# Gate scores of the second batch: as multiplying sums on VectorE from h, in place of matrix products on TensorE

## The chip, the cores and the metric

The kernel runs on one core of a Trainium2 chip. The metric is the device time of one launch, in microseconds (us), as the median of several runs. A core has TensorE (matrix products, written to PSUM), VectorE, ScalarE and GpSimd (elementwise work), SyncE (which issues transfers) and 16 DMA engines that all queues share. Every engine works through its own instructions strictly in order and waits on semaphores for the others. In the views of the profile, PE is TensorE, PEld its weight load, DVE VectorE, ACT ScalarE, POOL GpSimd and SP SyncE.

## What is computed

The input is x of shape (2, 1024, 256): two batches of 1024 rows, all in float32. There are two layers, each with a residual and a layer normalisation without weights behind it: a causal attention with one head of width 256, and a block with a 16-head causal attention (head width 128, rotary embedding) and a mixture of four experts. The part that matters here, cut from the reference (a, h, m of the second block):

```python
h = hidden_states + a
m = _moe(_layernorm(h, ln2_w, ln2_b), w_gate, we1, be1, we2, be2)
...
x = h.reshape(-1, d)                       # the normalised rows
raw = jax.nn.softmax(x @ w_gate, axis=-1)  # w_gate: 256 x 4
top_vals, top_idx = jax.lax.top_k(raw, TOP_K)
w = jax.nn.softmax(top_vals, axis=-1)
comb = jnp.zeros((t, E), x.dtype).at[jnp.arange(t)[:, None], top_idx].add(w)
hmid = jax.nn.gelu(jnp.einsum('td,edi->tei', x, we1) + be1[None], approximate=False)
eout = jnp.einsum('tei,eid->ted', hmid, we2) + be2[None]
out = jnp.einsum('te,ted->td', comb, eout)
```

So each of the 2048 rows has four gate scores, one for each expert; its two best experts are chosen by them, and the weights of the experts are held in comb (zero for the two that are not chosen). All four experts are computed for every row.

## The kernel before

Rows are worked in tiles of 128 (on the 128 partitions), eight tiles to a batch b. Half a batch (four tiles) is called j. The rows of h stand in one large tile (hx in the profile, 16 tiles of 128x256); the transposed, normalised rows stand in xT (called x2T in this part), features on the partitions.

**Order.** The body does not emit instructions at once. Each piece of work is a named call (`hidden 1 0 0` is `hidden` for batch 1, half 0, expert 0) that is put into a list; at the end the table MOVES (L28 to 299) takes single names out and puts them ahead of other names, and the list is then emitted. No scheduler works behind this: the order of the list is the order in every engine's queue. `at(s + 5, f)` puts a call into the step s + 5 of the attention's rows, of which s is the first of the last sixteen.

**The mixture of experts.** For half a batch the calls are: `m_stats` and `m_rstd` (mean, variance and 1/deviation of each row of h), `m_norm` (the normalised rows; on VectorE for batch 1, L498), `m_transposed` (four transposes on TensorE to PSUM, then ln2_w and ln2_b applied on the way to x2T: feature half c = 0 by ScalarE, L509, c = 1 by VectorE, L507), `gate_products`, `gate`, `gate_best`, `gate_weights` (from scores to comb), `hidden` for each expert (eight products of 512 columns into two PSUM banks, each then taken by a Gelu on ScalarE, L1693), `all_of` (16 products with we2 for one expert and four tiles, each tile then added to h with its weight from comb, VectorE, L1717), `m_bias` (the experts' second biases by the same instruction from SBUF, VectorE, L1672) and `m_residual` (adds x1 to h, GpSimd, L1577).

`hidden` uses two PSUM banks in turn, so that the next `hidden` can begin only when the Gelu of the one before has emptied the bank. ScalarE has to load a table when it goes from Exp or Ln to Gelu and back (ACT_TABLE_LOAD).

**The gate.** `gate_products` (L1586) makes, for each tile, two products of the transposed rows with w_gate, 128 columns by 4, and copies the scores of two tiles from PSUM with VectorE (L1601). `gate` (L1617) takes the largest score of a row, subtracts it and takes the exponential on ScalarE (L1625); `gate_best` finds the best and second best expert, and for the second takes another exponential on ScalarE (L1652); `gate_weights` writes comb. For batch 1 the four `gate_products` stand in two groups: tiles 0 to 3 behind `hidden 0 1 0`, tiles 4 to 7 behind `hidden 0 1 3`, and behind these come `gate 1`, `gate_best 1 0`, `gate_best 1 1`, `hidden 1 0 0`, `all_of 0 1 2`, `gate_weights 1`, `all_of 0 1 3`, `hidden 1 0 1`.

**The end of the attention.** The rotary tables stand in rope_sb (128 x 2 x 1024) and are used by GpSimd (L834 to L836) up to the last projection. For the last attention rows, VectorE transposes blocks of the softmax rows (L662), SyncE gathers them with 16 transfers of 128 KB (L673) into the tile pT, and TensorE multiplies them with the values (L1209). On GpSimd's own DMA queue, `load_second` (L1509) loads the last expert's we2 (256 KB, L1511) and be2, spread to all partitions (512 KB, L1513).

Of the kernel before, what the change touches and what calls it, by code (L numbers as in the profile page):

```python
# [12 lines left out]
F32 = mybir.dt.float32  # L13
AF = mybir.ActivationFunctionType
ALU = mybir.AluOpType
# [3 lines left out]
P = 128  # L19
# [13 lines left out]
    ("o_stats 1 0 0.1.2.3", "hidden 1 1 1"),  # L33
    ("hidden 1 0 3", "o_finish 0 0 0.1.2.3"),
    ("hidden 1 0 0", "all_of 0 1 2"),
    ("gate_products 1 6.7", "gate_products 1 4.5"),
    ("m_norm 1 1", "m_residual 0 0.1.2.3"),
    ("m_rstd 1 4.5.6.7", "m_norm 1 1"),
# [273 lines left out]
def kernel(  # L312
# [27 lines left out]
    nc = tc.nc  # L340
    B, S, D = x.shape
    DC = D // P
    NT = S // P
# [6 lines left out]
    E, I = be1.shape  # L350
# [63 lines left out]
    mpool = ctx.enter_context(tc.tile_pool(name="mpool", bufs=1))  # L414
# [49 lines left out]
    rope_sb = const.tile([P, 2, S], F32, name="rope_sb")  # L464
# [9 lines left out]
    h = hx.rearrange("p (n d) -> p n d", d=D)  # L474
# [648 lines left out]
    class RowB:  # L1123
# [45 lines left out]
        def place(self, j):  # L1169
            return (blocks_b if units.index(self.u) else blocks_a)[j]  # L1170
# [99 lines left out]
    def at(step, f, *args):  # L1270
        place(fills, step, f, args)
# [4 lines left out]
    def mid(step, f, *args):  # L1276
        place(mids, step, f, args)
# [113 lines left out]
    for k, (g, b) in enumerate(pairs):  # L1391
# [3 lines left out]
        wide = 0 < k < len(pairs) - 1  # L1395
# [90 lines left out]
    pools = {}  # L1486
# [52 lines left out]
    mv_h = [mpool.tile([P, NT, 2], F32, tag=f"mvh{b}", name="mvh") for b in range(B)]  # L1539
    rstd_h = [mpool.tile([P, NT], F32, tag=f"rsh{b}", name="rsh") for b in range(B)]  # L1540
# [3 lines left out]
    def table():  # L1544

        if other:
            nc.scalar.preload_act_table_set(TABLE)
            other.clear()
# [34 lines left out]

    pgs = {}

    def gate_products(b, tiles):  # L1586

        if tiles[0] == 0:
            pgs[b] = small.tile([P, NT, E], F32, tag="lg", name="lg", bufs=2)
        pg = ps_tr.tile([P, 512], F32, tag="tr", name="pg")  # L1590
        for i in tiles:
            for c in range(DC):
                nc.tensor.matmul(
                    pg[:, ts(i, E)],
                    lhsT=x2T[:, c, ds(b * S + i * P, P)],
                    rhs=wgate_sb[:, c, :],
                    start=(c == 0),
                    stop=(c == DC - 1),
                )
        lo, n = tiles[0], len(tiles)  # L1600
        nc.vector.tensor_copy(  # L1601
            pgs[b][:, lo : lo + n, :],
            pg[:, lo * E : (lo + n) * E].rearrange("p (n e) -> p n e", e=E),
        )

    def t3(tag):
        return small.tile([P, NT, E], F32, tag=tag, name=tag, bufs=2)

    def t2(tag):
        return small.tile([P, NT], F32, tag=tag, name=tag, bufs=2)  # L1610

    def wide(v):
        return v.unsqueeze(2).to_broadcast([P, NT, E])
# [3 lines left out]
    def gate(b):  # L1617

        lg = pgs[b]
        m = t2("gm")  # L1620
        nc.vector.tensor_reduce(m, lg, AX.X, ALU.max)
        nc.vector.tensor_tensor(lg, lg, wide(m), ALU.subtract)
        raw = t3("raw_g")
        table()
        nc.scalar.activation(raw, lg, AF.Exp)  # L1625
        raws[b] = raw
# [129 lines left out]
    s = A0 + (len(units) - 2) * NT  # L1756
    ST0, ST1, NM0, NM1 = 0, 2, 1, 3
    MT, GP0, H0 = (5, 6, 7, 8), (9, 9, 10, 11), 8
    GT = (11, 11, 12, 13)
    at(s + ST0, m_stats, 0, J0)  # L1760
    at(s + ST1, m_stats, 0, J1)
    at(s + NM0, m_rstd, 0, J0)
# [5 lines left out]
    for k in range(4):  # L1768
        at(s + GP0[k], gate_products, 0, (2 * k, 2 * k + 1))
    mid(s + H0, hidden, 0, 0, 0)  # L1770
    at(s + GT[0], gate, 0)
    at(s + GT[1], gate_best, 0, 0)
    at(s + GT[2], gate_best, 0, 1)
    at(s + GT[3], gate_weights, 0)
    for k in range(3):
# [27 lines left out]
    do(all_of, 0, 0, 2)  # L1803
    do(hidden, 0, 1, 0)
    do(gate_products, 1, (0, 1))
    do(gate_products, 1, (2, 3))
    do(all_of, 0, 0, 3)
    do(steps[end - 1].output, END)
# [19 lines left out]
    do(gate_products, 1, (4, 5))  # L1828
    do(gate_products, 1, (6, 7))
    do(gate, 1)  # L1830
    do(gate_best, 1, 0)
    do(gate_best, 1, 1)
# [84 lines left out]
```

## Time and profile before

| what | before |
|---|---|
| median of 3 runs | 1163.07 us (1158.52 to 1164.13) |
| the profiled execution | 1165.19 us, of which 1163.4 us is the span from the first to the last instruction |
| granted TensorE clock, mean | 0.994 of full speed |
| TensorE busy | 1133.0 us, 97% |
| VectorE busy | 852.5 us, 73% |
| GpSimd busy | 789.5 us, 68% |
| ScalarE busy | 648.7 us, 56% |
| gate products (L1593), both batches | 64 products of 128x128 by 128x4 |

Times within the profile count from the first instruction. The score products of the attention end at about 1031 us and its last output products at about 1078; the experts fill TensorE's time from 1039 on, and the calls of the gate for batch 1 lie between 1060 and 1106. A timeline line gives start, duration, engine, source line, operation, the tile written and those read with their shapes, how many instructions, and in brackets the idle time before and what ended it. The duration of several instructions reaches from the start of the first to the end of the last. A recorded duration overlaps the next instruction's start by up to 0.1 us, so that the distance of starts is the better price. A windows line gives, after the length of the window, the busy time of TensorE, its weight load, VectorE, ScalarE and GpSimd, each with a count in brackets, then the granted clock of TensorE, the mean busy share of the DMA engines, and GB/s. In the DMA view, q1 is SyncE's queue and q0 is GpSimd's.

### The profile page before, as it was taken

How to read it: one execution, taken by the hardware profiler on the slowest of the kernel's cores; microseconds unless marked ns; L12 is line 12 of the kernel's file. 1: busy time of each engine (PE TensorE's matmuls, PEld its weight loads, DVE VectorE, ACT ScalarE, POOL GpSimd, SP SyncE). 2: the span in 40 equal slices, each digit the busy share in tenths (PEclk: the TensorE clock that was granted, in tenths of full speed). 3: DMA queues.
4: the chain of work that ended last, by engine and by line, in shares of the span. 5: the costliest groups of instructions: out<-in, count | busy, mean ns of one | idle time of the engine just before them, and what ended most of it. 6: DMA issues, size and time to landing. Idle time of an engine off the chain costs nothing.

```text
span 1163.4 us, 15802 instructions
## 1 busy us (share of the span) xinstructions
PE 1133.0 (97%) x4628; PEld 718.6 (62%) x4628; DVE 852.5 (73%) x1813; ACT 648.7 (56%) x1228; POOL 789.5 (68%) x749
## 2 busy tenths in 40 slices
PE   8999989999999999999999999999999999999997
PEld 5666636656565656565757475756566656566765
DVE  5667797868686868687877778777868677575675
ACT  3333676665656565656566656565565656553444
POOL 4005999989897979697878868797989897002100
PEclk9999999999999999999999999999999999899999
DMA  6132465665546454555555545564555657405011
GB/s 187 36 88 57 117 174 140 135 138 125 127 113 130 107 138 110 118 122 131 119 125 131 131 112 131 132 138 115 132 129 128 148 121 180 106 15 145 1 37 36
DMA packets 243221, 133.89 MB, mean 115 GB/s; under 512 B 18908, under 2 KB 241184, under 8 KB 242368
## 3 DMA queue, kind: packets, MB, share of 16 engines
q1 hardware_dynamic: 238096, 123.02, 45.6%
q0 software_dynamic: 1776, 4.89, 1.6%
q10 hardware_dynamic: 3264, 4.98, 1.2%
q8 instruction: 37, 0.61, 0.2%
q14 instruction: 48, 0.39, 0.1%
HBM read 22.71 MB, written 4.19 MB: 23 GB/s over the span
## 4 chain that ended last, share of the span: by engine, by line
PE 87%; DVE 8%; DMA 2%; issue 1%; SPq 1%; ACT 1%; POOL 0%; DVEq 0%; ACTq 0%; POOLq 0%
PE sc L1143 19%; PE av L1209 19%; PE pa L919 10%; PE pa L1067 5%; PE pa L910 5%; PE pa L1685 5%; PE pe L1708 4%; PE pc L919 4%; PE pa L741 2%; PE sc L692 2%; PE pc L1067 2%; PE pc L910 2%; PE pa L599 1%; PE pa L586 1%; PE pa L1019 1%
## 5 line engine op out<-in xcount | busy, mean ns | idle before, releaser
L1160 ACT ACTIVATE pr<-pr,rs 128x128 f32<-128x128 f32 (+3 forms) x252 | 195.6, 778 | 188.9 <-DVE rs L1158 188.9
L1143 PE MATMUL sc<-Twk,Twq 128*128 128x512 f32 (+3 forms) x768 | 289.5, 487 | 4.3 <-ACT pr L624 4.3
L624 ACT ACTIVATE pr<-sc,nmx 128x640 f32<-128x640 f32 (+7 forms) x272 | 200.9, 739 | 154.4 <-DVE nmx L619 121.6
L1209 PE MATMUL av<-pT,vg 128*128 128x512 f32 (+3 forms) x768 | 271.0, 490 | 4.7 <-DMA pT<-pair_sb 2.4
L834 POOL TENSOR_TENSOR rot<-Twk,rope_sb 64x512 f32<-64x512 f32 x128 | 167.6, 1309 | 92.2 <-DVE Twk L952 70.0
L1209 PEld LDWEIGHTS av<-pT,vg 128*128 128x128 f32 x768 | 143.5, 191 | 128.6 <-issue 99.3
L619 DVE TENSOR_REDUCE nmx<-sc 128x1 f32<-128x640 f32 (+7 forms) x272 | 206.1, 758 | 9.4
L1143 PEld LDWEIGHTS sc<-Twk,Twq 128*128 128x128 f32 x768 | 135.6, 191 | 123.9 <-issue 108.7
L834 POOL TENSOR_TENSOR rot<-Twq,rope_sb 64x512 f32<-64x512 f32 x128 | 166.3, 1300 | 8.8
L617 DVE TENSOR_TENSOR sc<-sc,limit 128x128 f32<-128x128 f32 x272 | 79.2, 291 | 99.6 <-PE sc L1143 84.0
L662 DVE STREAM_TRANSPOSE x<-pr 128x640 f32<-128x640 f32 (+1 forms) x124 | 128.4, 1036 | 19.6 <-ACT pr L1160 11.9
L835 POOL TENSOR_TENSOR Twk<-Twk,rope_sb 128x512 f32<-128x512 f32 x64 | 85.8, 1341 | 5.0
L836 POOL TENSOR_TENSOR Twk<-Twk,rot 128x512 f32<-128x512 f32 x64 | 85.5, 1336 | 5.0
L835 POOL TENSOR_TENSOR Twq<-Twq,rope_sb 128x512 f32<-128x512 f32 x64 | 83.1, 1298 | 5.0
L836 POOL TENSOR_TENSOR Twq<-Twq,rot 128x512 f32<-128x512 f32 x64 | 82.0, 1281 | 5.0
L1577 POOL TENSOR_TENSOR hx<-hx,x 128x256 f32<-128x256 f32 x16 | 11.5, 745 | 90.1 <-DVE hx L1717 82.7
L662 DVE STREAM_TRANSPOSE pair_sb<-pr 128x128 f32<-128x128 f32 (+1 forms) x120 | 60.2, 502 | 8.0 <-ACT pr L1160 7.8
L1685 PE MATMUL pa<-xT,we_flat 128*128 128x512 f32 x128 | 59.6, 611 | 0.8 <-DVE hx L1029 0.8
L1076 DVE TENSOR_TENSOR hx<-hx,pa 128x512 f32<-128x512 f32 x70 | 46.6, 680 | 13.6 <-PE pa L1067 13.5
L1225 ACT ACTIVATE aT_sb<-av,par 128x512 f32<-128x512 f32 x64 | 43.8, 684 | 21.3 <-PE av L1209 19.8
L1708 PE MATMUL pe<-lent,hT 128*128 128x256 f32 x240 | 54.2, 379 | 0.0
L624 ACT ACTIVATION_READ_ACCUMULATOR pr<-sc,nmx 128x1 f32 x272 | 53.4, 196 | 0.0
(215 smaller groups left out, 1810.5 us busy)
## 6 DMA issues: line engine op xcount, KB each, us to landing
pT<-x SPq DMA_DIRECT2D x496, 128.0 KB, 2.7
pT<-pair_sb SPq DMA_DIRECT2D x480, 64.0 KB, 2.0
pT<-aT_sb SPq DMA_DIRECT2D x48, 128.0 KB, 2.7
pT<-za SPq DMA_DIRECT2D x48, 64.0 KB, 2.1
wk_g<-in_L_ffn_wk_dram SPq DMA_DIRECT2D x9, 256.0 KB, 3.0
wq_g<-in_L_ffn_wq_dram SPq DMA_DIRECT2D x9, 256.0 KB, 3.1
wv_g<-in_L_ffn_wv_dram SPq DMA_DIRECT2D x9, 256.0 KB, 3.1
wo_g<-in_L_ffn_wo_dram SPq DMA_DIRECT2D x9, 256.0 KB, 2.9
```

Source lines behind the costliest of these rows:

```text
L619: nc.vector.tensor_reduce(nmx, sc[:, :L], AX.X, ALU.max, negate=True)
L624: nc.scalar.activation(pr[:, :L], sc[:, :L], AF.Exp, bias=nmx, accum_out=sm)
L662: nc.vector.transpose(z[:, i % 4, :n, :], pr[:, : n * 32].rearrange("p (m s) -> p m s", s=32))
L834: nc.gpsimd.tensor_tensor(rot[lo, :], t[hi, cs], rope_sb[hi, 1, cs], ALU.mult)
L835: eng.tensor_tensor(t[:, cs], t[:, cs], rope_sb[:, 0, cs], ALU.mult)
L836: nc.gpsimd.tensor_tensor(t[:, cs], t[:, cs], rot, ALU.add)
L919: nc.tensor.matmul(pa, lhsT=w, rhs=x, start=start, stop=True, skip_group_check=True)
L1143: nc.tensor.matmul(sc[:, ds(n0, n)], lhsT=qT[:, ts(i, P)], rhs=kT[:, ds(n0, n)], start=True, stop=True,)
L1160: nc.scalar.activation(self.pr[:, :L], self.pr[:, :L], AF.Copy, scale=rs)
L1209: nc.tensor.matmul(cut(av), lhsT=vg[g, b][:, c, ts(hh, HD)], rhs=cut(pT[:, c, :]), start=(c == 0), stop=(c == i),)
L1685: nc.tensor.matmul(ph, lhsT=we1_sb[:, e, c, ts(m, P)], rhs=x2T[:, c, ds(k0 * P, 512)], start=(c == 0), stop=(c == DC - 1),)
L1708: nc.tensor.matmul(pe[:, ts(n, D)], lhsT=hTs[b, j, e][:, c, ts(k, P)], rhs=we2_sb[e][:, c, :], start=(c == 0), stop=(c == IC - 1),)
```

## The change

For batch 1, the scores of a row are made on VectorE from h itself. With g = ln2_w times w_gate (one row of 256 for each expert, on every partition) and c = the sum of ln2_b times w_gate, the score is rstd x (sum over d of (h - mean) x g) + c. The first factor and c are applied in `gate`. Batch 0 stays as it was.

```diff
+    ("gate_products 1 4.5", "m_residual 1 4.5.6.7"),
     ("gate_products 1 6.7", "gate_products 1 4.5"),
...
+    gw, g_raw = (rope_sb[:, k, :] for k in range(2))
+    cst = mpool.tile([P, E], F32, name="cst")
+    g_ln = []
+
+    def gate_loads():
+        nc.gpsimd.dma_start(g_raw, w_gate.rearrange("d e -> (d e)").partition_broadcast(P))
+        t = pools["l"].tile([P, 2, D], F32, tag="part", name="ln_rows", bufs=2)
+        for k, v in enumerate((ln2_w, ln2_b)):
+            nc.gpsimd.dma_start(t[:, k, :], v.partition_broadcast(P))
+        g_ln.append(t)
+
+    def gate_rows(e):
+        raw = g_raw.rearrange("p (d e) -> p e d", e=E)[:, e, :]
+        t = g_ln[0]
+        nc.gpsimd.tensor_tensor(gw[:, ts(e, D)], raw, t[:, 0, :], ALU.mult)
+
+        nc.vector.scalar_tensor_tensor(
+            g_junk, raw, 1.0, t[:, 1, :], ALU.mult, ALU.mult, accum_out=cst[:, e : e + 1]
+        )
+
+    g_junk = mpool.tile([P, D], F32, name="g_junk")
+
     def gate_products(b, tiles):
...
+        if b:
+
+            for i in tiles:
+                for e in range(E):
+                    nc.vector.scalar_tensor_tensor(
+                        g_junk, h[:, b * NT + i, :], mv_h[b][:, i, 0:1], gw[:, ts(e, D)],
+                        ALU.subtract, ALU.mult, accum_out=pgs[b][:, i, e : e + 1],
+                    )
+            return
...
     def gate(b):
 
         lg = pgs[b]
+        if b:
+            nc.vector.tensor_tensor(lg, lg, wide(rstd_h[b]), ALU.mult)
+            nc.vector.tensor_tensor(
+                lg, lg, cst.unsqueeze(1).to_broadcast([P, NT, E]), ALU.add
+            )
...
+    at(s + 5, gate_loads)
+    for e in range(E):
+        at(s + 7, gate_rows, e)
```

The order of the instructions of each engine, as built: TensorE loses 32 products. VectorE has 16 of the new instructions behind L1717 of `all_of 0 0 2` (tiles 0 to 3), and 16 behind L1717 of `all_of 0 1 1` (tiles 6, 7, 4, 5), ahead of L507 of `m_transposed 1 1 1` and of `gate 1`; each waits for the one before it, because all write g_junk. Before, L507 stood first there, and `m_residual 1 4.5.6.7`, which on GpSimd overwrites the h of those tiles, ran ahead of the gate products; it now stands behind them. The four sums for cst stand on VectorE behind the softmax maximum (L619) of the last full row of 1024, near 995 us in the profile before. GpSimd's three new loads (512, 128 and 128 KB) stand behind its `m_norm` of batch 0 (L498) and ahead of L1511 and L1513, its four products behind these. The loads write where the rotary tables were, and a buffer that the seven-product scheme used (tag part).

## Prediction, made before the changed kernel was run

> **What bounds the kernel.** I read the busy table and the chain of work that ended last, then the last 180 us on the timelines of TensorE, ScalarE and VectorE, the chain there, the DMA view in 2 us stretches, and the windows with the granted clock.
>
> ```profile
> PE 1133.0 (97%) x4628; PEld 718.6 (62%) x4628; DVE 852.5 (73%) x1813; ACT 648.7 (56%) x1228; POOL 789.5 (68%) x749
> ...
> PE 87%; DVE 8%; DMA 2%; issue 1%; SPq 1%; ACT 1%; POOL 0%; DVEq 0%; ACTq 0%; POOLq 0%
> ```
>
> TensorE is 97% busy and makes 87% of the chain. So a microsecond of TensorE counts in full, unless something else is then late. The second batch's gate scores stand on TensorE's timeline (start, duration):
>
> ```profile
> 1060.51 1.84 PE L1593 MATMUL pg<-wgate_sb,xT 128*128 128x4 f32 x16
> 1062.21 3.70 PE L1708 MATMUL pe<-lent,hT 128*128 128x256 f32 x16
> ...
> 1092.88 1.84 PE L1593 MATMUL pg<-wgate_sb,xT 128*128 128x4 f32 x16
> 1094.58 3.68 PE L1685 MATMUL pa<-xT,we_flat 128*128 128x512 f32 x8
> 1098.10 7.07 PE L1708 MATMUL pe<-lent,hT 128*128 128x256 f32 x32
> 1105.00 7.03 PE L1685 MATMUL pa<-xT,we_flat 128*128 128x512 f32 x16
> ```
>
> Each group holds TensorE for 1.70 us (1060.51 to 1062.21, 1092.88 to 1094.58), with no idle time behind it.
>
> **Removed: 2 x 1.70 = 3.40 us of TensorE**, and four copies of 0.17 us on VectorE, which sat waiting for them.
>
> **The new sums.** 32 SCALAR_TENSOR_TENSOR of 128x256 with an accumulated output. The trace has none with an accumulator. Nearest rows: eight of L1672 (128x256, two inputs in SBUF, each waiting for the one before, as the new ones do through the shared g_junk) take 4.00 us, 0.50 each; L1717 (one input in PSUM) is spaced by 0.415. ScalarE's accumulator is a record of its own, after which the next instruction starts 0.09 us later (992.33 to 992.42). I take 0.50 + 0.10 = **0.60**. Bounds: 0.415, and 0.50 + 0.42 = 0.92 if the sum were a pass of its own (L619 over 256 elements is 0.42). 0.60 is close to L1672, the same instruction but for the accumulator.
>
> A rule speaks against the change. The Trainium skill, "Vector Engine (DVE) Microarchitecture Reference", section "Points that are easy to get wrong", says that this instruction runs at half throughput with two SBUF sources that aren't bf16, as no read port is left for the accumulator. L1672, with two such sources but no accumulator, shows 0.50 against 0.415, no halving; whether the accumulator brings it, no row here shows. By the rule each would be some 0.25 to 0.30 us dearer, an estimate from that page, and 16 of them 4 to 5 us.
>
> In the second group, VectorE also runs m_norm 1 1 without GpSimd's additions beside it (four took 1.37 us at 1049.40, alone, and 2.20 at 1081.85, beside them); it then waits for TensorE anyway, so this brings nothing.
>
> **First group (tiles 0 to 3), gain kept.** VectorE is free at 1057.28 + 1.57 = 1058.85. 16 x 0.60 = 9.6, to 1068.4; then L1717 (1.57) and eight L1672 (up to 4.5), to 1074.5. The next on VectorE (L1029, 1076.70 now, 1075.0 then) waits for TensorE. Cover 0.5 us; beyond it there are 4.5 us more, as the transposes of 1088.57 need the normalised tiles ready at 1084.05. Row: **-1.70**. GpSimd's residual additions there (0.745 each) start some 1 to 2 us later and are needed only at 1084.
>
> **Second group (tiles 4 to 7), gain lost.** Here the gate itself is behind the sums, and ScalarE takes its exponentials ahead of the next Gelu:
>
> ```profile
> 1095.40 0.23 ACT L1625 ACTIVATE raw_g<-lg 128x32 f32<-128x32 f32 x1 [0.34 <-DVE lg L1622]
> 1098.88 0.21 ACT L1652 ACTIVATE e<-e 128x8 f32<-128x8 f32 x1 [3.25 <-DVE e L1650]
> 1099.11 1.28 ACT L1693 ACT_TABLE_LOAD   x1
> 1100.40 1.27 ACT L1693 ACTIVATE hT<-pa,par 128x512 f32<-128x512 f32 x2
> ```
>
> The first Gelu ends at 1100.40 + 0.69 = 1101.09 and frees the accumulator bank that TensorE's hidden 1 0 1 takes at 1105.00: 3.9 us of slack. Afterwards: L1717 of all_of 0 1 1 starts 1.70 earlier, 1087.07, and ends 1088.64; sums to 1098.24; L507 (0.73) to 1098.97; the two new small operations (0.22 each, like L1622) to 1099.41. There the gate begins, against 1094.96: 4.45 later. So the Gelu ends at 1105.54, while TensorE wants the bank at 1105.00 - 3.40 = 1101.60. **Stall 3.94 us**, in place of a gain of 1.70 here. Each 0.1 us in the price of a sum is 1.6 us of stall.
>
> The clock reacts to such an idle spell. Windows of 3.41 us (last columns clock, DMA share, GB/s):
>
> ```profile
> 930.15:933.57 3.42, 1.02 (x4) 0.23 (x3) 0.27 (x2) 0.16 (x2) 3.28 (x3) 1.00 0.79 158
> 933.57:936.98 3.41, 3.41 (x5) 1.35 (x6) 2.25 (x5) 2.01 (x3) 3.19 (x4) 0.50 0.37 84
> ...
> 988.18:991.59 3.41, 1.11 (x3) 0.49 (x3) 0.89 (x2) 0.17 (x1) 0.00 (x0) 1.00 0.19 36
> 991.59:995.00 3.41, 2.59 (x4) 0.83 (x3) 1.80 (x5) 1.54 (x3) 0.00 (x0) 0.50 0.00 0
> 995.00:998.42 3.42, 3.42 (x5) 1.35 (x4) 1.92 (x3) 2.30 (x4) 0.00 (x0) 0.50 0.41 97
> ```
>
> After a window in which TensorE was busy for a third, the next ones run at 0.50 until one was full. 3.94 us of idle time leaves at least one window less than half busy: 3.41 us at half clock, **+1.71**. Second group: -1.70 + 3.94 + 1.71 = **+3.95**.
>
> GpSimd's m_residual 1 4 to 7 (3.0 us) now waits for the sums, to about 1098; nothing is queued behind it, and L1672 needs those tiles only after 1127.
>
> **The loads.** GpSimd issues three more DMAs ahead of we2 and be2 at 982.37: 512 + 128 + 128 KB, 0.79 MB, as much as we2 and be2 together. (Issue costs 0.6 to 0.8 us each on GpSimd, idle until 1066 otherwise; its four products, 0.745 each, lie there too.) What it meets, in the chain and in the DMA view of 981 to 983, then of 985 to 987 (packets, MB):
>
> ```profile
> 983.68 2.38 DMA pT<-x
> 986.06 4.39 issue
> 990.45 0.05 DVEq L662
> 990.55 0.84 DVE x L662
> ```
> ```profile
> q1 hardware_dynamic: 881, 0.43, 118.2%
> ```
> ```profile
> q0 software_dynamic: 135, 0.49, 90.2%
> q1 hardware_dynamic: 93, 0.04, 9.9%
> ```
>
> SyncE's gather for the attention rows goes at 0.43 MB in 2 us alone, and at 0.04 beside GpSimd's queue. Its last part lands at about 990.4; TensorE waits for it from 988.38 to 990.67, and through L662 and L1029 again until 994.33. At GpSimd's 0.49 MB in 2 us, 0.79 MB more is **3.2 us** of delay (bounds: none, if the gather gets its turn; 4). TensorE: L1209 at 993.87, four at half clock to 997.3, hidden 0 0 0 at 997.53 in place of 994.33. There the half clock now covers 991.59 to 998.42; the eight matmuls take 5.71 us against 3.43 at full clock. Later on, the clock is back between 997.3 and 1000.7; taking 999.0, they end at 1001.7, not 1000.03: **+1.7** (0.9 to 2.5).
>
> New waits: the first sum for cst waits on VectorE for these loads, with the transposes and reciprocals of the last attention rows queued behind it; we2 and be2 land 4.6 and 6.7 us after their issue, so loads issued from 982.4 to 984.2 should be there by about 991, before 995.90, when VectorE comes to it. GpSimd's products wait for the same loads, and nothing behind them is due before 1066. we2 and be2 themselves land 3 us later and are first read after 1023. The four sums for cst (2.4 us, behind L619 at 995.90) have VectorE's 3.6 us of idle time before 1000.51; with both shifts they just fit. Without that cover up to 2 us of ScalarE's work comes late, and it idles 5 us in the next 10. I add nothing.
>
> **Sum:** +1.7 - 1.7 + 3.95 = **+3.95**. On the profiled execution (1165.19, of which 1163.40 is span) that is 1169.1; that execution lies 2.1 above the median, so I forecast 1163.07 + 3.95 = **1167.0**. A measurement tells apart about 0.5%, 5.8 us.
>
> **Rivals.**
> - Forecast, a stall behind the gate and a later gather eat the gain: +1.5 to +6.5, chance 0.45 (same 0.37, slower 0.08).
> - Sums near 0.85: 13.6 us each group. The gate begins at 1103.4, the Gelu ends at 1109.5, the stall is 7.9: 1.7 - 1.7 - 1.7 + 7.9 + 1.7 = +7.9, 1171.0. Slower by over 0.5% from 0.72 on (16 x 0.12 = 1.9 more). For it: two SBUF inputs and an accumulator, unseen here. Against it: L1672. 0.25 (slower 0.22, same 0.03).
> - The gather isn't delayed further (it gets turns, as from 987 on, when q1 recovers while q0 still moves): +2.2, 1165.3; 0.15, same.
> - Sums at 0.415: gate at 1096.45, stall 1.0, clock stays: -1.7 - 0.7 = -2.4, plus 0 to 0.9 of the gather: 1160.7 to 1161.6; 0.15 (same 0.13, faster 0.02). Even with no stall the gain is 3.4, so faster by 5.8 needs luck in the clock.
>
> Faster 0.02, same 0.68, slower 0.30. The range takes the rivals in: 1160.7 to 1171.8.
>
> **What would show it.** The accumulating instructions' spacing (0.60); TensorE idle some 4 us before hidden 1 0 1, released by ScalarE's Gelu, with a 0.50 window behind it; TensorE's wait for pT near 990 grown from 2.3 to 5.5 us; no idle time at the first group. Wrong if the sums cost 0.42 or 0.9, or if the gather lands as before.

## The result, and the profile after

The changed kernel takes 1168.05 us (median of 6 runs, 1166.54 to 1170.89), the kernel before 1161.21 in the same comparison (6 runs, 1158.31 to 1164.13): ratio 1.0056, 95% interval 1.0039 to 1.0073. A second comparison gave 1168.34 against 1162.99: 1.0041, interval 1.0027 to 1.0055. So, by the ratios, the change costs some 4.8 to 6.5 us. The forecast was +3.95 us. The profiled execution took 1168.01 us, its span 1166.1.

The busy table of the changed kernel, and its chain of work by engine:

```profile
PE 1131.4 (97%) x4596; PEld 714.9 (61%) x4596; DVE 871.1 (75%) x1883; ACT 648.6 (56%) x1228; POOL 794.3 (68%) x756
...
PE 86%; DVE 8%; DMA 2%; ACT 1%; issue 1%; SPq 1%; POOL 0%; ACTq 0%; DVEq 0%; POOLq 0%
```

TensorE has 32 products less but only 1.6 us less of busy time, and VectorE has 18.6 us more. (Line numbers are now those of the changed kernel: L1724 is `hidden`, L1747 and L1756 are the products and the additions of `all_of`, L1732 is the Gelu.) On TensorE's timeline of the changed kernel the gate products are gone, and an idle spell stands in brackets:

```profile
1087.14 7.03 PE L1724 MATMUL pa<-xT,we_flat 128*128 128x512 f32 x16
1094.01 7.07 PE L1747 MATMUL pe<-lent,hT 128*128 128x256 f32 x32
1105.03 9.72 PE L1724 MATMUL pa<-xT,we_flat 128*128 128x512 f32 x16 [3.95 <-ACT hT L1732]
1114.59 3.62 PE L1747 MATMUL pe<-lent,hT 128*128 128x256 f32 x16
```

The first line is `hidden 0 1 3` and `hidden 1 0 0`, now without gate products between them, and the second follows at once. But `hidden 1 0 1` (third line, with `hidden 1 0 3` behind it) waits 3.95 us for ScalarE's Gelu, and the 16 products of these two take 9.72 us where the 16 of the first line take 7.03. ScalarE in the same stretch:

```profile
1099.29 0.23 ACT L1664 ACTIVATE raw_g<-lg 128x32 f32<-128x32 f32 x1 [6.53 <-DVE lg L1661]
1102.77 0.21 ACT L1691 ACTIVATE e<-e 128x8 f32<-128x8 f32 x1 [3.25 <-DVE e L1689]
1103.00 1.28 ACT L1732 ACT_TABLE_LOAD   x1
1104.29 1.26 ACT L1732 ACTIVATE hT<-pa,par 128x512 f32<-128x512 f32 x2
```

ScalarE waits 6.53 us for the scores (0.34 before). Its four steps have the same lengths as before, all 3.89 us later; the first Gelu empties the bank at 1104.29 + 0.69 = 1104.98, and TensorE starts at 1105.03. VectorE, which makes the scores:

```profile
1088.05 0.48 DVE L1619 SCALAR_TENSOR_TENSOR g_junk<-hx,mvh,rope_sb 128x256 f32<-128x256 f32 x1
1088.45 0.08 DVE L1619 DVE_READ_ACCUMULATOR g_junk<-hx,mvh,rope_sb 128x1 f32 x1
1088.57 0.48 DVE L1619 SCALAR_TENSOR_TENSOR g_junk<-hx,mvh,rope_sb 128x256 f32<-128x256 f32 x1
...
1094.39 1.05 DVE L1619 SCALAR_TENSOR_TENSOR g_junk<-hx,mvh,rope_sb 128x256 f32<-128x256 f32 x1
1096.95 0.81 DVE L508 TENSOR_SCALAR xT<-pt,par 128x512 f32<-128x512 f32 x1
1097.68 0.22 DVE L1655 TENSOR_TENSOR lg<-lg,rsh 128x32 f32<-128x32 f32 x1
1097.93 0.65 DVE L1656 TENSOR_TENSOR lg<-lg,cst 128x32 f32<-128x32 f32 x1
```

Each sum is an instruction of 0.48 us and a read of its accumulator of 0.08; two sums start 0.52 apart (1088.05 to 1088.57). The 16 take 8.90 us (to 1096.95). One of them takes 1.05 us, with a GpSimd addition (1094.43 to 1095.15) beside it. The windows of the changed kernel behind the stall (as before: TensorE, weight load, VectorE, ScalarE, GpSimd, then clock, DMA share, GB/s):

```profile
1100.04:1103.45 3.41, 1.04 (x5) 0.57 (x3) 3.03 (x16) 0.66 (x2) 0.00 (x0) 1.00 0.00 0
1103.45:1106.87 3.42, 1.84 (x2) 0.84 (x3) 3.32 (x14) 2.10 (x3) 0.00 (x0) 0.50 0.00 0
1106.87:1110.28 3.41, 3.41 (x5) 1.35 (x4) 3.20 (x8) 0.69 (x1) 0.00 (x0) 0.50 0.00 0
1110.28:1113.69 3.41, 3.41 (x9) 1.52 (x8) 0.55 (x2) 1.30 (x2) 0.00 (x0) 1.00 0.00 0
```

A window busy for 30% is followed by one at 0.50; that one is busy for 54%, and the next stays at 0.50; only after a full one is the clock back.

Near 990, where the last gather is awaited, the wait on the changed kernel's TensorE timeline is 3.21 us (2.29 before), and its DMA view of 985 to 987 shows SyncE's gather (q1) beside GpSimd's loads (q0):

```profile
990.95 3.58 PE L1210 MATMUL av<-pT,vg 128*128 128x512 f32 x4 [3.21 <-issue]
```
```profile
q0 software_dynamic: 120, 0.39, 73.3%
q1 hardware_dynamic: 321, 0.16, 33.0%
```

**The end of the program by stretches.** To compare kernels I cut TensorE's timeline at fixed calls, from the start of one to the start of the next. The stretches repeat to about 0.1 us, except where the clock or the gather enters:

| stretch (us) | before | change | again | e2 | e3 | e4 | e5 | e6 | e8 | e9 | e10 |
|---|---|---|---|---|---|---|---|---|---|---|---|
| first group: `hidden 0 1 0` to `0 1 1` | 14.26 | 12.48 | 12.47 | 12.48 | 12.48 | 12.48 | 12.48 | 12.48 | 12.48 | 12.47 | 12.48 |
| second group: `hidden 0 1 3` to `1 0 0` | 5.14 | 3.44 | 3.44 | 5.14 | 3.44 | 3.43 | 3.44 | 3.44 | 3.43 | 3.44 | 3.44 |
| stall: `hidden 1 0 0` to `1 0 1` | 10.42 | 14.46 | 14.46 | 10.42 | 10.34 | 14.46 | 10.34 | 12.46 | 21.16 | 14.46 | 10.34 |
| clock: `hidden 1 0 1` to `1 0 2` | 10.32 | 13.01 | 13.20 | 10.32 | 11.13 | 12.12 | 11.12 | 12.12 | 13.26 | 10.42 | 10.32 |
| sum of these, less before | 0 | +3.25 | +3.43 | -1.78 | -2.75 | +2.35 | -2.76 | +0.36 | +10.19 | +0.65 | -3.56 |
| median less before's (us) | | +6.8 | +5.4 | +1.8 | +0.1 | +4.1 | -2.7 | +1.2 | +9.1 | +1.6 | -4.4 |

e1, e7 and e11 have the values of before in all four rows. In e3 and e5 the clock row holds the 0.5 us of idle time before `hidden 1 0 3`, not a half clock. From `hidden 1 0 2` to the last product it is 41.50 in every kernel. The differences of medians are uncertain by 1.5 to 2 us each.

### The profile page after: what moved, and what is told of

The parts are those of the page before. It is cut to its first block, busy times and chain, and to the rows that moved or that the text cites. A ratio compares the mean times of both kernels' runs of the same rounds, so it can differ in the third digit from the quotient of the medians.

```text
span 1166.1 us, 15821 instructions
## 1 busy us (share of the span) xinstructions
PE 1131.4 (97%) x4596; PEld 714.9 (61%) x4596; DVE 871.1 (75%) x1883; ACT 648.6 (56%) x1228; POOL 794.3 (68%) x756
## 4 chain that ended last, share of the span: by engine, by line
PE 86%; DVE 8%; DMA 2%; ACT 1%; issue 1%; SPq 1%; POOL 0%; ACTq 0%; DVEq 0%; POOLq 0%
PE sc L1144 19%; PE av L1210 19%; PE pa L920 10%; PE pa L1068 5%; PE pa L911 5%; PE pa L1724 4%; PE pc L920 4%; PE pe L1747 4%; PE pa L742 2%; PE sc L693 2%; PE pc L1068 2%; PE pc L911 2%; DMA pT<-x 1%; PE pa L600 1%; PE pa L587 1%; PE pa L1020 1%
## 5 line engine op out<-in xcount | busy, mean ns | idle before, releaser
L1724 PE MATMUL pa<-xT,we_flat 128*128 128x512 f32 x128 | 60.0, 616 | 4.0 <-ACT hT L1732 4.0
L1747 PE MATMUL pe<-lent,hT 128*128 128x256 f32 x240 | 54.1, 379 | 0.0
```

The lines of the kernel that those rows point to most:

```text
L1724: nc.tensor.matmul(ph, lhsT=we1_sb[:, e, c, ts(m, P)], rhs=x2T[:, c, ds(k0 * P, 512)], start=(c == 0), stop=(c == DC - 1),)
L1747: nc.tensor.matmul(pe[:, ts(n, D)], lhsT=hTs[b, j, e][:, c, ts(k, P)], rhs=we2_sb[e][:, c, :], start=(c == 0), stop=(c == IC - 1),)
```

## The experiments

**My theory:** the gate, put off by VectorE's sums, holds ScalarE's exponentials, which hold the Gelu queued behind them, which holds TensorE's bank; the stall and the half clock behind it give back more than the removed products bring. The loads add some microseconds at the gather. **Rivals:** the loads alone make the loss; or the sums slow VectorE in the first group too; or the long idle spell matters only through the clock.

**The loads and the sums for cst alone (e1).** In `gate_products` and `gate`, batch 1 goes the old way; the new row of the order is taken out:

```diff
-        if b:
+        if b > 1:
...
```

> The new loads, GpSimd's four products and VectorE's four sums for cst alone; all gate scores by TensorE as before (gw and cst aren't read). Theory of the gate stall (the exponentials ahead of the Gelu cost it all): 0 to +2 us against the kernel before, no TensorE idle time between 1060 and 1110. Rival (the loads delay the gather near 990 us): +3 to +5 us, most of the change's +6.8.

Measured: 1163.87 against 1162.14, ratio 1.0013 (1.0001 to 1.0025), that is +0.1 to +2.9 us. All four stretches of the table are those of before. So the loads are not the main loss.

**The new sums in the first group only (e2).** Tiles 4 to 7 get their scores from TensorE again:

```diff
-        if b:
+        if b and tiles[0] < 4:
...
```

> Loads as in the change, tiles 0 to 3 by VectorE, tiles 4 to 7 by TensorE as before. Theory of the gate stall: 1.7 us less than the run with the loads alone, no idle time ahead of hidden 1 0 1. Rival (the sums weigh on VectorE wherever they stand): no faster than the loads alone, TensorE waits for VectorE after 1070.

Measured: 1163.94 against 1162.14, 1.0011 (0.9997 to 1.0025). In the stretches the first group gains 1.78 us and nothing is given back there. The time doesn't show that gain beside e1 (1.0013): the intervals are as wide as the gain, and e2's profile has a longer wait at the gather, on TensorE's timeline of e2:

```profile
991.65 3.75 PE L1209 MATMUL av<-pT,vg 128*128 128x512 f32 x4 [5.46 <-issue]
```

**The Gelu ahead of the gate's exponentials (e3).** One row more in the table of the order:

```diff
+    ("hidden 1 0 0", "gate 1"),
```

> The change with hidden 1 0 0 put ahead of gate 1, so that its Gelus stand ahead of the gate's exponentials on ScalarE; the order of TensorE and VectorE is the same. Theory of the gate stall: the 3.95 us of idle time before hidden 1 0 1 shrink to about 0.5 (before hidden 1 0 3), no window at half clock there, about 6 us faster than the change, 1161 to 1163. Rival (the loads): the stall goes or not, but the time stays above 1164.

Measured: 1162.25 against 1162.14, 0.9994 (0.9976 to 1.0011). The sums are as late as in the change. On TensorE's timeline of e3, `hidden 1 0 1` starts without a wait, and 0.54 us of idle time remain ahead of `hidden 1 0 3`:

```profile
1100.09 3.60 PE L1725 MATMUL pa<-xT,we_flat 128*128 128x512 f32 x8
1104.22 3.70 PE L1725 MATMUL pa<-xT,we_flat 128*128 128x512 f32 x8 [0.54 <-ACT hT L1733]
```

So it is the order on ScalarE that turns late scores into a stall of TensorE.

**The loads later, on SyncE's queue (e4).** The loads stand ahead of a later score row, and the sums for cst and GpSimd's products ahead of `all_of 0 0 0`:

```diff
+    ("gate_loads", "RowB.scores 270"),
+    ("gate_rows 0", "all_of 0 0 0"),
...
-        nc.gpsimd.dma_start(g_raw, w_gate.rearrange("d e -> (d e)").partition_broadcast(P))
+        nc.sync.dma_start(g_raw, w_gate.rearrange("d e -> (d e)").partition_broadcast(P))
...
```

> The change with its three loads on SyncE's queue behind the gather and wo of 1007 to 1019 us, and the products and the sums for cst ahead of all_of 0 0 0 (VectorE idle there for 2.8 us). Theory of the gate stall: as the change, within 2 us, the stall of 4 us still there. Rival (the loads near 990): 3 to 5 us faster than the change.

Measured: 1166.26 against 1162.14, 1.0042 (1.0026 to 1.0058): hardly better than the change. Its stall is the same 3.95 us. The wait for the gather is 1.80 us in its profile.

**Both (e5): e3's and e4's edits.**

> The change with hidden 1 0 0 ahead of gate 1 and the loads late on SyncE, both as in the runs before. Gate stall and loads are separate and add up: -3.4 us of products, +0.5 of stall, nothing near 990 us: 2.5 to 3 us faster than the kernel before (-0.2 to -0.3%). Rival (TensorE's 3.4 us are eaten elsewhere too): as the run with the Gelu first alone, about the kernel before.

Measured: 1160.33 against 1163.01, 0.9978 (0.9965 to 0.9991): faster than before. The stretches sum to -2.76, the median says -2.7.

**Half of the second group's sums earlier (e6).** Tiles 6 and 7 go ahead of `all_of 0 1 1`, into idle time of VectorE; nothing else is changed:

```diff
+    ("gate_products 1 6.7", "all_of 0 1 1"),
```

> The change, with the sums of tiles 6 and 7 ahead of all_of 0 1 1's additions, where VectorE idled for 1.83 us; ScalarE's order as in the change. If VectorE's chain sets the stall one for one: stall 3.95 - 1.85 = about 2.1 us before hidden 1 0 1, one window at half clock or none, 3.5 to 4.5 us faster than the change. Rival (the stall hangs on something else of ScalarE's): 3.95 us as before.

Measured: 1164.17 against 1163.01, 1.0005 (0.9990 to 1.0021). On TensorE's timeline of e6 the stall is 2 us shorter:

```profile
1105.32 8.83 PE L1725 MATMUL pa<-xT,we_flat 128*128 128x512 f32 x16 [1.96 <-ACT hT L1733]
```

This joins the two ends of the chain: what VectorE is earlier (some 1.8 us of its idle time are used), TensorE's wait is shorter.

**A control: the kernel before with the Gelu first (e7)**, e3's row alone, without the change.

> Control: the kernel before with hidden 1 0 0 ahead of gate 1, all scores by TensorE. Theory of the gate stall: the kernel before has 3.9 us of slack there, so no difference, within 1 us. Rival (that order is better by itself): 2 us or more faster than the kernel before.

Measured: 1162.16 against 1163.01, 0.9987 (0.9973 to 1.0002), all stretches as before. There the gate wasn't late, so its order brought nothing that the interval tells from zero; e3's gain is the stall of the change.

**The idle spell filled with products (e8).** The change, with products of 128x4 into a tile that nobody reads, ahead of `hidden 1 0 1`. There are 32 calls of 128x128 by 128x4; each float32 call is recorded as two products, so that the filler, meant to be 3.4 us long, has 64 of them and took 10.96:

```diff
+    def fill():
...
     do(all_of, 0, 1, 3)
+    do(fill)
     do(hidden, 1, 0, 1)
```

> The change with 32 products of 128x128 by 128x4 (3.4 us, written to a PSUM tile that nothing reads) ahead of hidden 1 0 1, in the stall: TensorE's idle time there shrinks to 0.5 us, but hidden 1 0 1 can begin no earlier. If the clock falls because of the idle time: no half clock after 1103, 1.7 to 3.4 us faster than the change although TensorE has more to do. Rival (no clock cost): as the change.

Measured: 1172.12 against 1163.01, 1.0073 (1.0055 to 1.0091). The filler was too long to test the time, but its profile shows something else. Windows of e8 (the small products run from 1100.02 to 1110.85, then `hidden 1 0 1`):

```profile
1099.60:1103.00 3.40, 3.40 (x31) 3.35 (x29) 3.09 (x15) 1.10 (x2) 0.00 (x0) 0.99 0.00 0
1103.00:1106.40 3.40, 3.40 (x18) 3.40 (x18) 3.26 (x14) 1.66 (x3) 0.00 (x0) 0.50 0.00 0
```

TensorE is recorded as busy throughout, and yet the clock falls to 0.50 behind the first window, and stays there for 13.65 us, the last 5.8 of them with `hidden`'s wide products. So "no idle time, no half clock" doesn't hold.

**The spell filled with wide products (e9):** four calls of 128x128 by 128x512 (eight products as recorded), in place of e8's 32.

```diff
+    def fill():
...
     do(all_of, 0, 1, 3)
+    do(fill)
     do(hidden, 1, 0, 1)
```

> The change with eight recorded products of 512 columns (3.43 us, into a PSUM tile that nothing reads) in the stall ahead of hidden 1 0 1, in place of the small products of the run before, which were twice as many as meant. If the clock goes by the columns that stream through the array: no half clock after 1103, hidden 1 0 1 still begins where the Gelu lets it, and the stretch from there to hidden 1 0 2 falls from 13.0 to 10.3 us; 1.8 to 2.7 us faster than the change. If the half clock comes from something else: as the change.

Measured: 1164.63 against 1162.99, 1.0019 (1.0004 to 1.0034); the change, repeated beside it, 1.0041. TensorE's timeline of e9, the filler and then `hidden 1 0 1`, at full speed (7.13 us against 9.72):

```profile
1097.31 3.60 PE L1644 MATMUL pg<-xT,we_flat 128*128 128x512 f32 x8
1101.43 7.13 PE L1736 MATMUL pa<-xT,we_flat 128*128 128x512 f32 x16 [0.52 <-ACT hT L1744]
```

`hidden 1 0 1` starts as late as in the change (14.46); only the clock differs, and the next stretch is 10.42 in place of 13.01 to 13.20. So the half clock is a cost of its own beside the stall, 2.6 to 2.8 us here.

**All three mends (e10):** e5's and e6's edits together.

> Late loads, the Gelu first, and the sums of tiles 6 and 7 ahead of all_of 0 1 1: the last 0.5 us of stall before hidden 1 0 3 go too. 3 to 4 us faster than the kernel before, 0.5 to 0.8 faster than the run without the split. Rival (something else is late by then): as the run without the split.

Measured: 1158.56 against 1162.99, 0.9961 (0.9946 to 0.9977): some 4.4 us faster than before, and 9.8 less than the change repeated beside it. TensorE's timeline of e10 has neither idle time nor half clock there:

```profile
1091.73 7.07 PE L1754 MATMUL pe<-lent,hT 128*128 128x256 f32 x32
1098.64 7.03 PE L1731 MATMUL pa<-xT,we_flat 128*128 128x512 f32 x16
1105.51 3.62 PE L1754 MATMUL pe<-lent,hT 128*128 128x256 f32 x16
```

**The loads early, the sums for cst late (e11):** e1, with the four `gate_rows` moved as in e4.

```diff
+    ("gate_rows 0", "all_of 0 0 0"),
...
```

> All scores by TensorE; the loads near 982 us as in the change, but the four sums for cst ahead of all_of 0 0 0. If the sums cost the 1.25 us that the stretch from hidden 0 0 0 to hidden 0 1 0 grew in the run with loads and sums, it is 57.04 again and the time falls by that; what is left against the kernel before is the gather's, 0 to 1 us. If the loads cost it, the stretch stays at 58.3.

Measured: 1161.87 against 1162.99, 0.9998 (0.9981 to 1.0015). By this the early loads cost nothing that shows (at most 1.7 us), though e11's own profile has a wait of 5.57 us at the gather. That profile is of the slowest of the twelve executions (1166.86, median 1161.87), so its wait is not the usual one.

**The change repeated (e12).**

> The change once more, to see which of its stretches are the same in every execution: the stall of 3.95 us and both gains of 1.7 should be there to 0.1 us; the gather near 990 us and the number of windows at half clock may differ.

Measured: 1168.34 against 1162.99, 1.0041 (1.0027 to 1.0055). Its profile has the same stall (3.96) and two windows of half clock behind it.

## Why the prediction was right in the main, step by step

- **Removed products, -1.70 each:** measured -1.78 and -1.70. Right. The cover of the first group held: VectorE still waited 0.93 us for TensorE behind the sums (0.5 predicted).
- **Price of a sum, 0.60:** measured 0.53 as the usual spacing, 0.82 to 1.05 where a GpSimd addition ran beside it. The 16 took 8.90, not 9.60. But the two small operations behind them took 0.93, not 0.44 (the second alone 0.65, beside GpSimd's `m_residual`). The two errors nearly cancel: the gate begins 12.14 us after the start of `all_of 0 1 1`'s additions (L1756), against 12.34 predicted.
- **The rule against two SBUF sources** (the Trainium skill, "Vector Engine (DVE) Microarchitecture Reference", section "Points that are easy to get wrong"): not borne out here. By the median the instruction takes 485 ns with its accumulator; L1672, with two SBUF sources and none, takes 485 too, and L1717, with one source in PSUM, 476. Nothing is halved; the measurement decides.
- **Stall, 3.94:** measured 3.95 by the idle time in brackets, +4.04 by the distance of starts in the table (on TensorE a recorded duration overlaps the next start by up to 0.17 us: 1098.10 + 7.07 against 1105.00 before). e3 and e6 show that its cause is the one named: the late gate, through ScalarE's order. The agreement to 0.1 us is luck in part: the sums were 0.70 us cheaper than predicted, but the two small operations behind them 0.49 dearer, and from the gate's start to ScalarE's exponential it took 0.68 us in place of 0.44.
- **Clock, +1.71:** right in kind, too small. It was worked out from one window at half clock. The change shows two, and +2.69 and +2.88; e4 and e6 show one, and +1.80. How many there are depends on how the idle spell lies to the windows: the second one stays at half when the first is only 54% busy (65% in the repeated change); in e4 and e6 the first is full, and the next is at full clock. Half the busy time of the two windows, (1.84 + 3.41) / 2 = 2.63 us, is nearly all of the +2.69.
- **The loads, +1.7:** the size may be right, but it isn't settled, and the mechanism was only half right. I let the whole 0.79 MB pass ahead of the gather; the DMA view shows the gather moving 0.16 MB beside 0.39. In the change's profile the wait grew by 0.92 us, not 3.2. Over nine profiles with early loads it is 1.7 to 5.6 us (mean 3.1), over five without 1.8 to 2.6 (mean 2.1). From the start of the last score product ahead of the wait to `hidden 0 1 0`, the nine take 67.9 to 71.6 us (mean 69.5), the five 66.7 to 69.3 (mean 67.5); and what the medians in the table hold beyond the four stretches is on average +1.5 us with early loads and 0.0 without. So the averages speak for 1.5 to 2 us. Single comparisons don't agree: the times of e11 (no cost, up to 1.7) and of e4 (hardly a gain) speak against it, those of e5 against e3 (-1.9 us) for it. The sum also took the half clock of 991.59 to 998.42 as given: of the five profiles without early loads only that of the kernel before has it there; e4, e5, e7 and e10 have none.
- **"I add nothing" for the sums for cst:** that failed in part. In the profiles of the change, e1, e3 and e9 the stretch from the end of `hidden 0 0 0` to `hidden 0 1 0` is 58.28 to 58.29 us, 1.24 more than in the kernel before and in e4, e5, e10 and e11, where these sums stand later. In e6, e8 and the repeated change it is 57.04 with the sums early. The clock parts the two groups: in the first, `hidden 0 0 0` runs at full clock and takes 3.51 us to the next product; in the second it runs at half clock and takes 5.4 to 5.7, some 2 us more of cover for VectorE (e2 lies between, 4.48 us and +0.25). The prediction counted on that cover from one execution, and the change's profile didn't have it. Part of the cost is seen as a wait of 0.59 us for ScalarE's xT at 1008.
- **The sum:** -1.78 - 1.70 + 4.04 + 2.69 = +3.25 at the end of the program, where the prediction had -1.70 + 3.95 = +2.25. The other +1.4 to +3.2 (the two ratios, less +3.43 and +3.25) lie in what the last two points leave open, or in the clock's one or two windows from run to run; the runs don't part these.

The rival that came nearest was the dear sums (slower by over 0.5%): the time is near that bound, but not for its reason.

## What to carry to other kernels

Before work is moved from the engine that sets the end to one with idle time, follow the result to its reader, and then what is queued behind that reader: here scores that were 4 us late held an exponential, the exponential held a Gelu of other data, and the Gelu held TensorE's bank. The mend is in the order, not in the operation: with the Gelu first, half of the sums earlier and the loads out of the way, the same change gains 4.4 us in place of losing about 5. A stall of TensorE can bring windows of half clock on top: here one or two for 2 to 4 us at the end, none for 0.5 us (e3, e5). At the gather, waits of 1.7 to 2.6 us brought none in seven profiles (e1, e3, e4, e5, e7, e9, e10) and two in the kernel before (2.3), e8 (2.8) and the repeated change (2.0), so that the sum needs both cases.

## What the runs showed of the hardware

- The busy time of the profile isn't what the clock follows. A window recorded as 100% busy, all but its first 0.4 us with back-to-back products of 128x4, was followed by 13.65 us at 0.50 (e8); products of 512 columns in the same place kept 1.00 (e9). The Trainium skill, "TensorE: Matmul & The Clock Gate", section "Part 1: The HAM clock gate (the "warmup" mystery)", says that the gate follows how busy the array has been lately; the drop after a window that was 30% busy agrees; e8 shows that the recorded busy time isn't the measure of it.
- With GpSimd's additions beside them, some of VectorE's instructions took longer: a sum 0.82 to 1.05 us in place of 0.48, an operation of 128x32 0.65 in place of 0.22. Not all did: the 128x32 product just before (L1655, 1097.68) ran beside them in 0.22.
- The four sums for cst, whose first source is read with a stride of four elements, took 0.60 to 0.63 us each, where the others take 0.48; that the stride is the reason was not tested.
